# A decoder layer with soft experts on one core: unread products in TensorE's waits before the first expert, and one more copy for ScalarE

## The chip, the cores and the metric

The kernel runs on one core of a Trainium2 chip. The core has TensorE (PE, matrix products; its weight loads are listed apart as PEld), VectorE (DVE), ScalarE (ACT), GpSimd (POOL) and SyncE (SP, which issues most DMAs). Each works through its own queue in order, and they wait for each other through semaphores. The metric is the device time of one execution in microseconds (us), the median of several runs. Before the change it is 2900.55 us over 3 runs (2897.71 to 2901.32).

## The reference

A pre-norm decoder layer on x of 32 sequences x 100 tokens x 256 channels in float32, with a context of 361 tokens for each sequence:

```python
x = x + attn(layernorm(x))            # 16 heads of 16, rotary, causal
x = x + xattn(layernorm(x), ctx)      # 16 heads of 16, with biases, over 361 context tokens
x = x + ffn(layernorm(x))

# ffn: 8 experts of 128 slots each; two token softmaxes over the same logits
xn, sn = rmsnorm(x), rmsnorm(slot_embeds)
logits   = einsum('bnd,esd->bnes', xn, sn)
dispatch = softmax(logits, axis=tokens)
combine  = softmax(logits, axis=all 1024 slots)
slots = einsum('bnd,bnes->besd', xn, dispatch)
h     = gelu(einsum('besd,edh->besh', slots, w1) + b1)      # 256 -> 1024
eo    = einsum('besh,ehd->besd', h, w2) + b2                # 1024 -> 256
out   = einsum('bmd,bnm->bnd', eo, combine)
```

## The kernel before

The 32 sequences form 8 groups of 4 (SIZES). For each group and each of the 8 experts, `run_expert` computes `ph` (first layer, 16 products of 128x512), `hT` (gelu on ScalarE), `pe` (second layer, 32 pieces of products of 128x256) and `py` (the combination). While the experts of group g run, the attention work of group g+1 is threaded between their products. Group 0 has no experts to hide behind: its self attention, cross attention, logits and routing run alone ahead of the first `ph`. That is the part in which this change acts.

The order of all queues is written out when the program is built, by a planner inside the kernel. `pe["t"]` is its own clock for TensorE. `matmul` and `transpose` emit a product and call `spend`, which adds an estimated duration to `pe["t"]`, multiplied by `pe["slow"]`: 1.25 until group 0 is prepared, 1.0 behind that. Work for the other engines is queued as jobs (`vec`, `act`, `gps`, and `job("SP", ...)` for transfers) with an estimated duration, what they read and what they write. `run` emits every job that can start by `pe["t"]`, choosing by start time, priority and place in its list. The attention work is written as generators (`self_attention`, `cross_softmax`, `crossing`, `cross_queries`, `cross_context`, `prepare`, `slots`); each yields a `Need` with the tiles and PSUM banks that its next piece waits for. `drive` takes the next piece that fits; if none does, it calls `advance`, which moves `pe["t"]` on to the next event: that is a wait of TensorE as the planner sees it. `hold` does the same for a bank or tile that is needed at once.

PSUM: two score pairs, `sc0` and `sc1` (the ring "pairs", each of two banks of 512 columns; line 310), take turns for the score products of both attentions and for the transposed logits `ps_l` (line 1512). Self attention writes 400 columns of each bank, cross attention 361, `ps_l` all 512. Four single banks hold everything else until group 0 is prepared; after that they are split into two for attention and two for the experts (line 1805).

The names in the first part of the program, in the order of one sequence:

- `layer_stats` and `turned` (lines 659 and 692): bnst and bnmv on VectorE; ve, rstd and xh on POOL; `ps_xhT` transposes on TensorE, copied to xhT by ScalarE.
- self attention: `ps_qk` products, rope on VectorE and POOL (ropeu, ropet), rotk on ScalarE; score products sc<-rotk; p with the causal mask and nmax on VectorE, subtraction on POOL (line 891), exp on ScalarE (line 899); `ps_pT` transposes for group 0; `ps_av`, oT, `ps_o` into the residual x.
- context: `ps_cT` transposes, ctxT copies (ScalarE, line 1060), `ps_kT` products, kT (ScalarE, line 1076), `ps_xv` values into vpad (VectorE).
- cross attention in four "quads" for each sequence: score products sc<-kT,xqT into sc0 and sc1; xnmax on VectorE (line 1162, one reduction for each pair); exps on ScalarE (line 1172, two for each pair, each with an accumulator read). For group 0 (`early`) the exps go to p in SBUF, and `cross_turn` (line 1210) transposes p in three chunks of 128, 128 and 105 context tokens: 12 `ps_xpT` transposes for each quad, and one copy for each chunk into xpT. Chunk 1 is copied by ScalarE, chunks 0 and 2 by VectorE (line 1217). Later groups transpose through VectorE and a store and load in DRAM instead (xt, xd).
- `ps_rb`, `ps_xav`, xoT, `ps_o`; then `tokens` and `prepare`: `ps_lt` logits, `ps_l`, cnm, `ps_nm`; `soften` and `route`: pd, disp, sl, slT. Then the first `ph`.

The slot embeddings (se, 1 MB) are loaded at the start; eight squares on ScalarE (line 597), rn on POOL (line 603), a scaling on VectorE and 16 `ps_sn` transposes turn them into snT.

Of the kernel before, what the change touches and what calls it, by code (L numbers as in the profile page):

```python
# [23 lines left out]
def decoder_layer(ctx: ExitStack, tc: tile.TileContext, a: dict, out: bass.AP):  # L24
# [8 lines left out]
    nc = tc.nc  # L33
    x, cx = a["x"], a["ctx_1024"]
    B, S, D = x.shape
# [12 lines left out]
    HG = 4  # L48
# [28 lines left out]


    COL, PIPE, HOP, LOAD = 0.00084, 0.25, 0.15, 1.28
    pe = {"t": 0.0, "slow": 1.25}  # L80
    waiting = {e: [] for e in ("DVE", "ACT", "POOL", "SP")}
    idle_from = {"DVE": 0.0, "ACT": 3.0, "POOL": 5.0, "SP": 0.0}
    tables = {"now": None, "gelus": 0}
# [11 lines left out]
    class Buf:  # L95
# [2 lines left out]

        def __init__(self, make=None, prev=None, before=(), ap=None, root=None, psum=False):
            self.make, self.prev, self.before, self.ap, self.root = make, prev, before, ap, root  # L100
            self.psum = psum
            self.writes, self.uses = [], []

        def get(self):
# [86 lines left out]
    def ends(items):  # L191
        t = 0.0
        for i in items:
            e = i if isinstance(i, float) else i.end
            if e is None:
                return None
            t = max(t, e)
        return t
# [64 lines left out]
    def advance(*times):  # L263

        nxt = run()
        ahead = [t for t in (*times, nxt) if t is not None and t > pe["t"]]
        assert ahead, "nothing left that could go on"
        pe["t"] = min(ahead)

    def hold(items, fill=None):  # L270

        while True:
            run()
            t = ends(items)
            if t is not None and (t == 0.0 or t + HOP <= pe["t"]):
                return
            if fill is None or not fill():
                advance(None if t is None else t + HOP)

    def spend(cols, passes, share):  # L280
        pe["t"] += passes * (COL * cols / share + (0.012 if share > 1 else 0.0)) * pe["slow"]
# [15 lines left out]
    class Banks(Ring):  # L297
# [6 lines left out]
        def tile(self, name):  # L304
# [4 lines left out]
    rings = {  # L309
        "small": Banks([(ps_m, "mm"), (ps_b, "big")]), "big": None,  # L310
        "pairs": Kept(
            [ps_s.tile([P, 2, 512], F32, tag=f"sc{i}", name=f"sc{i}") for i in range(2)], psum=True
        ),
    }
# [26 lines left out]
    def free(when):  # L341
        return Need(banks=0, when=when)
# [27 lines left out]
    def drive(goal, *streams):  # L370


        while goal.it:
            run()
            ready = [s for s in streams if s.fits()]
            if ready:
                min(ready, key=lambda s: s.need.seq).step()
            else:
                advance(*(s.time() for s in streams))
        return goal.result  # L380

    ident = const.tile([P, P], F32, name="ident")
# [827 lines left out]
    def cross_turn(xpT, p):  # L1210
        for ci, (k0, n) in enumerate(KC):
            yield Need(*p)
            ps = bank("ps_xpT")
            for q in range(NQ):
                transpose(ps.get()[:n, q * SQ : (q + 1) * SQ], p[q].get()[:, k0 : k0 + n], ident)
            mine = xpT.part()
            f = nc.scalar.copy if ci == 1 else nc.vector.tensor_copy
            job(
                "ACT" if ci == 1 else "DVE", 0.49 if ci == 1 else 0.57,
                lambda f=f, ps=ps, n=n, ci=ci: f(  # L1220
                    xpT.get()[:n, :, ci, :, :QN],
                    ps.get()[:n].rearrange("k (h g u) -> k g h u", h=NQ, u=QB)[:, :, :, :QN],
                ),
                [ps], [mine], prio=0,
            )
# [235 lines left out]
    def prepare(g):  # L1461

        nb, nt = SIZES[g], SIZES[g] * S
        nm, cs, diag = R["cnm"].new(), R["cs"].new(), R["diag"].new()
        for b0 in range(0, nb, 2):
            m = min(2, nb - b0)
            for i in range(b0, b0 + m):
                yield free(lambda: len(turning) > 0)  # L1470
                k, at = turning.pop(0)
                assert at == i
                yield Need(k.xns[i])
                transposed(
                    k.xns[i], lambda: k.xn.get()[:, i, :],
                    lambda i=i: k.xnT.get()[:, :, i * S : (i + 1) * S], k.xnT,
                )
            yield free(lambda: state["slots"].it is None and state["routed"] >= NE - 1)
            if b0 == 0:
                k.logits()  # L1480
            cols_ = slice(b0 * S, (b0 + m) * S)
            for e in range(0, NE, 2):
                yield Need(k.xnT, snT)
                ps = bank("ps_lt")
                pv = ps.get().rearrange("p (e n) -> p e n", e=2)[:, :, : m * S]
                for i in range(2):
                    for dc in range(ND):
                        matmul(
                            pv[:, i, :], lhsT=snT.ap[:, dc, (e + i) * NS : (e + i + 1) * NS],
                            rhs=k.xnT.get()[:, dc, cols_],  # L1490
                            start=(dc == 0), stop=(dc == ND - 1),
                        )
                lt = k.lt[e // 2]
                act(
                    0.5, lambda lt=lt, pv=pv: nc.scalar.copy(lt.get()[:, :, cols_], pv), [ps], [lt],
                    prio=0,
                )
                vec(
                    0.57,
                    lambda e=e, pv=pv, ps=ps, b0=b0, m=m: nc.vector.tensor_reduce(  # L1500
                        k.mx.get()[:, e : e + 2, b0 : b0 + m],
                        pv.rearrange("m e (b n) -> m e b n", b=m), axis=AX.X, op=ALU.max,
                    ),
                    [ps], [k.mx], prio=0,
                )

            for b in range(b0, b0 + m):
                if g > 0 and b0 + 2 < nb:
                    mine = logit_squares(k, b, nm, cs)
                else:  # L1510
                    yield Need(*k.lt, banks=0, pairs=1, exps=(1.4, 4.0))
                    ps = rings["pairs"].new("ps_l")
                    pv = ps.get().rearrange("n h s -> n (h s)")
                    for e in range(NE):
                        transpose(
                            pv[:S, e * NS : (e + 1) * NS],
                            k.lt[e // 2].get()[:, e % 2, b * S : (b + 1) * S], ident,
                        )
                    warm("exp")
                    mine = nm.part()  # L1520
                    vec(
                        1.2,
                        lambda b=b, pv=pv: nc.vector.tensor_reduce(
                            nm.get()[:, b : b + 1], pv[:S], axis=AX.X, op=ALU.max, negate=True
                        ),
                        [ps], [mine], prio=0,
                    )
                    act(
                        1.28,
                        lambda b=b, pv=pv: nc.scalar.activation(  # L1530
                            pv[:S], pv[:S], AF.Exp, bias=nm.get()[:, b : b + 1],
                            accum_out=cs.get()[:, b : b + 1],
                        ),
                        [ps, mine], [cs.part()], table="exp", prio=0,
                    )
                vec(
                    0.27,
                    lambda b=b: nc.vector.tensor_scalar(
                        diag.get()[:, b, :], ident[:S, :S], nm.get()[:, b : b + 1], None, ALU.mult
                    ),  # L1540
                    [mine], [diag],
                )
        k.ci = R["cinv"].new()
        vec(
            0.18, lambda: nc.vector.reciprocal(k.ci.get()[:, :nb], cs.get()[:, :nb]), [cs], [k.ci]
        )

        yield Need(diag)
        ps = bank("ps_nm")
        matmul(  # L1550
            ps.get()[:, :nt], lhsT=ones, rhs=diag.get()[:, :nb].rearrange("k b n -> k (b n)"),
            start=True, stop=True,
        )
        k.nmB = R["nmB"].new()
        act(
            0.49, lambda: nc.scalar.copy(k.nmB.get()[:, :nt], ps.get()[:, :nt]), [ps], [k.nmB], prio=0
        )
# [222 lines left out]
    pe["t"] = 1.5  # L1780
    run()
    rows, se = load_constants()
    make_constants()
    load_slots(se)
    slots_kept.append(se.kept())
# [12 lines left out]
    def order():  # L1798
        return (*streams[:2], steps, *streams[2:])
# [14 lines left out]

    routing = Steps(routes(groups[0], 0))
    ready = drive(routing, routing, *order())
    w = weights
    todo = [(g, e) for g in range(NG) for e in range(NE)]
    for i, (g, e) in enumerate(todo):
# [115 lines left out]
```

## Time and profile before

| | |
|---|---|
| median of 3 runs | 2900.55 us (2897.71 to 2901.32) |
| profiled execution | 2904.49 us, its span 2902.5 us |
| mean granted TensorE clock | 0.987 of full speed |
| TensorE busy | 2855.3 us, 98% of the span |
| VectorE, ScalarE, POOL busy | 1519.4, 1190.6, 557.3 us (52%, 41%, 19%) |
| DMA | 446.34 MB, mean 154 GB/s |

TensorE's share is a mean over a short first part, in which one group's attention runs alone, and a long second part of experts. The costliest groups of the page are all of the second part. The columns are line, engine, operation, output and inputs, shapes, count; busy time and mean of one; idle time ahead of them:

```profile
L290 PE MATMUL pe<-w,hT 128*128 128x256 f32 x4096 | 980.4, 383 | 0.0
L290 PE MATMUL ph<-slT,w 128*128 128x512 f32 x2048 | 965.7, 598 | 0.5
L1693 ACT ACTIVATE hT<-ph,cols 128x512 f32<-128x512 f32 x512 | 351.7, 687 | 816.2 <-PE ph L290 816.0
```

The two lines of TensorE have no idle time of note ahead of them. What ended TensorE's waits in the first 254 us (us in total, times, longest):

```profile
PE ps_xhT L294 <- POOL xh L698: 7.0, 5, 4.3
PE psWk L294 <- DMA rawWk<-in_L_attn_Wk_dram: 5.8, 1, 5.8
PE sc L290 <- ACT p L1172: 4.5, 6, 1.5
PE sc L290 <- DVE xt L1186: 2.8, 2, 2.6
PE ps_xpT L294 <- ACT pT L934: 2.2, 1, 2.2
PE ps_rb L294 <- DVE wide L715: 2.1, 1, 2.1
PE ps_xpT L294 <- ACT kT L1076: 2.1, 1, 2.1
PE sc L290 <- DVE xqT L1122: 2.1, 1, 2.1
```

The waits are spread over many causes: ScalarE, VectorE, POOL and the first transfers.

### The profile page before, as it was taken

The page shows a single profiled execution, that of the slowest core. Times are in us where ns is not written, and L with a number is a line of the kernel's source. Part 1 is how long each engine was busy: PE and PEld are TensorE (multiplying, and loading weights), DVE is VectorE, ACT ScalarE, POOL GpSimd, SP SyncE. Part 2 cuts the span into 40 slices and gives each one's busy share as a digit, 9 for nine tenths or more (in the row PEclk, how much of TensorE's full clock was granted, in tenths as well). Part 3 has the DMA queues.
Part 4 walks back from the last instruction along what each step waited for, and adds up shares of the span by engine and source line. Part 5 has one row for each costly group of instructions (what it writes and reads, how often), then busy time and mean ns, then how long its engine had stood idle before and what let it go on. Part 6 is the DMA issues. An engine that isn't in the chain of part 4 may idle for free.

```text
span 2902.5 us, 42479 instructions
## 1 busy us (share of the span) xinstructions
PE 2855.3 (98%) x16609; PEld 1982.1 (68%) x16609; DVE 1519.4 (52%) x2831; ACT 1190.6 (41%) x2538; POOL 557.3 (19%) x729
## 2 busy tenths in 40 slices
PE   7989999999999999999999999999999999999999
PEld 5765667676667676676667667677666766676676
DVE  5676565565455556456465465555555555423121
ACT  3544444443434434444443444434434434333331
POOL 4331321022210322112220211202221021100000
PEclk8988999999999999999999999999999999999999
DMA  3015564555554554555464464554555455533231
GB/s 109 11 50 181 175 214 147 190 165 173 167 184 152 188 171 155 185 171 178 154 204 158 141 218 148 192 184 139 185 177 175 163 182 171 175 93 100 78 98 53
DMA packets 331542, 446.34 MB, mean 154 GB/s; under 512 B 18280, under 2 KB 300880, under 8 KB 331344
## 3 DMA queue, kind: packets, MB, share of 16 engines
q1 hardware_dynamic: 330656, 442.90, 46.8%
q8 instruction: 132, 2.16, 0.3%
q10 hardware_dynamic: 688, 0.73, 0.1%
q14 instruction: 66, 0.54, 0.1%
HBM read 300.82 MB, written 142.74 MB: 153 GB/s over the span
## 4 chain that ended last, share of the span: by engine, by line
PE 92%; DMA 3%; DVE 3%; ACT 1%; POOL 1%; issue 1%; SPq 0%; ACTq 0%; DVEq 0%; POOLq 0%
PE pe L290 30%; PE ph L290 30%; PE sc L290 5%; PE sl L290 4%; PE py L290 4%; PE ps_lt L290 3%; PE ps_xv L290 3%; PE ps_xav L290 2%; PE ps_kT L290 2%; PE ps_o L290 2%; PE ps_qk L290 2%; PE ps_av L290 1%; PE ps_v L290 1%; PE ps_xq L290 1%; DMA xpT<-xd 1%; PE ps_xpT L294 1%
## 5 line engine op out<-in xcount | busy, mean ns | idle before, releaser
L290 PE MATMUL pe<-w,hT 128*128 128x256 f32 x4096 | 980.4, 383 | 0.0
L290 PE MATMUL ph<-slT,w 128*128 128x512 f32 x2048 | 965.7, 598 | 0.5
L290 PEld LDWEIGHTS pe<-w,hT 128*128 128x128 f32 x4096 | 751.6, 190 | 159.3 <-issue 50.2
L1693 ACT ACTIVATE hT<-ph,cols 128x512 f32<-128x512 f32 x512 | 351.7, 687 | 816.2 <-PE ph L290 816.0
L290 PEld LDWEIGHTS ph<-slT,w 128*128 128x128 f32 x2048 | 372.0, 190 | 314.7 <-issue 285.5
L1172 ACT ACTIVATE sc<-sc,xnmax 128x361 f32<-128x361 f32 x448 | 238.0, 531 | 175.6 <-DVE xnmax L1162 168.2
L1162 DVE TENSOR_REDUCE xnmax<-sc 128x2 f32<-128x722 f32 x256 | 221.5, 899 | 167.9 <-PE sc L290 167.5
L1186 DVE STREAM_TRANSPOSE xt<-sc 128x384 f32<-128x384 f32 x448 | 230.5, 554 | 21.5 <-ACT sc L1172 15.1
L1592 POOL TENSOR_TENSOR dT<-dT,ri 128x400 f32<-128x400 f32 x64 | 54.9, 858 | 964.8 <-DVE ri L1589 964.8
L891 POOL TENSOR_TENSOR p<-p,nmax 100x800 f32<-100x800 f32 x64 | 96.7, 1523 | 421.3 <-DVE nmax L884 404.5
L1747 DVE SCALAR_TENSOR_TENSOR x<-py,cinv,x 100x256 f32<-100x256 f32 x256 | 112.0, 475 | 115.5 <-PE py L290 114.9
L667 POOL TENSOR_SCALAR ve<-bnmv 100x1 f32<-100x1 f32 x96 | 23.2, 244 | 724.3 <-DVE bnmv L664 674.2
L1724 DVE TENSOR_TENSOR eo<-pe,b 128x512 f32<-128x512 f32 x128 | 87.2, 681 | 137.9 <-PE pe L290 137.1
L290 PE MATMUL sc<-kT,xqT 32*128 32x361 f32 x1024 | 130.5, 532 | 9.5 <-ACT p L1172 4.5
L290 PEld LDWEIGHTS sl<-disp,xn 100*128 100x128 f32 x1024 | 134.4, 192 | 7.2 <-ACT sc L1172 0.6
L290 PE MATMUL sl<-disp,xn 100*128 100x128 f32 x1024 | 135.1, 275 | 0.0
L290 PE MATMUL py<-eo,cT 128*100 128x256 f32 x512 | 131.5, 379 | 0.8 <-DVE eo L1724 0.8
L290 PEld LDWEIGHTS py<-eo,cT 128*100 128x100 f32 x512 | 85.5, 167 | 50.0 <-issue 27.2
L874 DVE TENSOR_TENSOR p<-sc,causal 100x800 f32<-100x800 f32 x64 | 60.4, 985 | 106.2 <-PE sc L290 106.1
L811 DVE STREAM_TRANSPOSE st<-p 128x1024 f32<-128x1024 f32 x56 | 113.6, 2029 | 0.1
L1660 DVE TENSOR_SCALAR slT<-sl,cols 128x512 f32<-128x512 f32 x128 | 93.2, 728 | 37.7 <-PE sl L290 37.7
L1241 DVE TENSOR_TENSOR xoT<-ps_xav,rb 128x100 f32<-128x100 f32 x64 | 16.7, 260 | 180.9 <-PE ps_xav L290 180.8
(155 smaller groups left out, 3243.4 us busy)
## 6 DMA issues: line engine op xcount, KB each, us to landing
w<-in_L_ffn_w_dram SPq DMA_DIRECT2D x512, 256.0 KB
xd<-xt SPq DMA_DIRECT2D x112, 768.0 KB
xpT<-xd SPq DMA_DIRECT2D x112, 768.0 KB
sd<-st SPq DMA_DIRECT2D x70, 512.0 KB
pT<-sd SPq DMA_DIRECT2D x70, 512.0 KB
dd<-dt SPq DMA_DIRECT2D x56, 256.0 KB
disp<-dd SPq DMA_DIRECT2D x56, 256.0 KB
ctx<-in_ctx_dram SPq DMA_DIRECT2D x32, 256.0 KB
```

The costliest lines, as they stand in the source:

```text
L290: nc.tensor.matmul(out, lhsT=lhsT, rhs=rhs, **kw)
L811: lambda: nc.vector.transpose(st.get().rearrange("p j h u -> p h j u"), p.get()[:, hs, :].rearrange("p h (u j) -> p h j u", j=4),),
L874: lambda i=i, hs=hs: nc.vector.tensor_tensor(p.get()[:S, hs, :S].rearrange("n (q h) k -> n q h k", q=2), sc[i].get()[:S, :, : HG * S].rear ...
L891: lambda hs=hs: nc.gpsimd.tensor_tensor(p.get()[:S, hs, :S], p.get()[:S, hs, :S], nmax.get()[:, hs].unsqueeze(2).to_broadcast([S, HPC, S]) ...
L1162: lambda nm=nm, sc=sc: nc.vector.tensor_reduce(nm.get(), sc.get()[:, :, :SK], axis=AX.X, op=ALU.max, negate=True),
L1172: nc.scalar.activation(to[:, :SK], sc.get()[:, i, :SK], AF.Exp, bias=nm.get()[:, i : i + 1], accum_out=sums.get()[:, c, q, r : r + 1],)
L1186: nc.vector.transpose(t_.get()[:, :, :, 2 * t + i, :].rearrange("p j c u -> p c j u"), sc.get()[:, i, : NKB * P].rearrange("p (c u j) -> p ...
L1592: lambda: nc.gpsimd.tensor_tensor(dT.get()[:, :nb, :S], dT.get()[:, :nb, :S], ri.get()[:, :nb].unsqueeze(2).to_broadcast([P, nb, S]), ALU. ...
L1660: lambda dc=dc, sl=sl: nc.vector.tensor_scalar(slT.get()[:, dc, : nb * NS], sl.get()[:, : nb * NS], cols.ap[:, NGM + dc : NGM + dc + 1], N ...
L1693: lambda h=h, ph_=ph_, hc=hc: nc.scalar.activation(h.get()[:, :n], ph_.get()[:, :n], AF.Gelu, bias=cols.ap[:, e * NHC + hc : e * NHC + hc ...
L1724: lambda eo=eo, po=po, m=m: nc.vector.tensor_tensor(eo.get()[:, :m], po.get().rearrange("p (i d) -> p i d", i=2)[:, :m], b2.get().unsqueez ...
L1747: lambda b=b, i=i: nc.vector.scalar_tensor_tensor(xs[g].get()[:, b, :], py[:S, i, :], k.ci.get()[:, b : b + 1], xs[g].get()[:, b, :], ALU. ...
```

## The change

Three things are changed.

1. From the moment the constants are made until the first expert's routing is done (`awake`), `advance` hands each planned wait to `keep_awake`. It adds the waits up, and for each 0.4 us of them emits one product of the identity with 112 columns of itself into columns 400 to 511 of the second bank of sc0. Nobody reads these columns, except `ps_l` and its reader; while such a use of sc0 is not over (`whole`), nothing is emitted.
2. `pe["slow"]`, the planner's factor on TensorE's durations in that part, is 1.06 where it was 1.25.
3. In `cross_turn`, which only the first group uses, chunks 0 and 1 are copied by ScalarE and chunk 2 by VectorE.

```diff
-    pe = {"t": 0.0, "slow": 1.25}
+    pe = {"t": 0.0, "idle": 0.0, "slow": 1.06}
...
-            self.psum = psum
+            self.psum, self.whole = psum, False
...
         assert ahead, "nothing left that could go on"
+        keep_awake(min(ahead) - pe["t"])
         pe["t"] = min(ahead)
+
+    def keep_awake(wait):
+
+
+        if not awake:
+            return
+        now = rings["pairs"].past[::2][-1:]
+        if now and now[0].whole and (ends(now[0].uses) or 1e9) > pe["t"]:
+            return
+        pe["idle"] += wait
+        while pe["idle"] > 0.4:
+            nc.tensor.matmul(
+                rings["pairs"].tiles[0][:, 1, HG * S :], lhsT=ident, rhs=ident[:, : 512 - HG * S],
+                start=True, stop=True,
+            )
+            pe["idle"] -= 0.4
...
+    awake = []
...
-            f = nc.scalar.copy if ci == 1 else nc.vector.tensor_copy
+            f = nc.scalar.copy if ci < 2 else nc.vector.tensor_copy
             job(
-                "ACT" if ci == 1 else "DVE", 0.49 if ci == 1 else 0.57,
+                "ACT" if ci < 2 else "DVE", 0.49 if ci < 2 else 0.57,
...
                     ps = rings["pairs"].new("ps_l")
+                    ps.whole = True
...
     rows, se = load_constants()
+    awake.append(True)
     make_constants()
...
     ready = drive(routing, routing, *order())
+    awake.clear()
     w = weights
```

## The prediction

> **What bounds the kernel now.** I read the page's shares and slices first, then a table by stage, then the places where TensorE ran at half clock, then the waits ahead of them. The slices (40 of 72.6 us each):
>
> ```profile
> PE   7989999999999999999999999999999999999999
> ...
> PEclk8988999999999999999999999999999999999999
> ```
>
> TensorE is short of 9 tenths, and its granted clock below full, in the first slices alone. The table by stage has, for each stretch, its length, then busy time of PE, weight loads, DVE, ACT and POOL, then the clock, DMA share and GB/s. The first row is everything up to the first expert's steady run, the second the rest:
>
> ```profile
> 0.00:254.00 254.00, 215.36 (x1719) 156.64 (x1720) 169.70 (x324) 114.52 (x316) 89.96 (x127) 0.86 0.24 75
> 254.00:2902.50 2648.50, 2639.92 (x14892) 1825.49 (x14890) 1349.69 (x2507) 1076.08 (x2222) 467.29 (x602) 1.00 0.49 161
> ```
>
> After 254 us TensorE idles 2648.50 - 2639.92 = 8.6 us at full clock. Nothing that this change does can gain there. Before it TensorE idles 254.00 - 215.36 = 38.6 us, and part of its busy time is at half clock. Half-microsecond windows give ten such stretches (length, PE busy, clock, DMA share, GB/s):
>
> ```profile
> 29.15:32.50 3.35, 3.01 (x6) 0.50 0.09 30
> 35.95:42.75 6.80, 6.28 (x33) 0.50 0.00 0
> 53.00:59.75 6.75, 6.12 (x31) 0.50 0.01 2
> 63.25:66.65 3.40, 2.86 (x14) 0.50 0.00 0
> 70.05:80.35 10.30, 10.30 (x36) 0.50 0.01 2
> 141.75:145.10 3.35, 3.35 (x20) 0.50 0.00 0
> 148.55:155.40 6.85, 6.85 (x24) 0.50 0.00 0
> 182.70:189.50 6.80, 5.89 (x65) 0.50 0.18 61
> 216.95:237.35 20.40, 17.56 (x76) 0.50 0.53 183
> 244.15:247.50 3.35, 3.29 (x50) 0.50 0.38 92
> sum 71.35, PE 65.50; mean PE 6.55
> ```
>
> The lengths are multiples of about 3.4 us: the clock is set by such windows. At full clock the 65.50 us would be 32.75. So 32.75 us is the most that a warm TensorE can give. The same work shows the ratio (8 products ps_qk each, cold, then warm):
>
> ```profile
> 56.79 1.92 PE L290 MATMUL ps_qk<-xhT,wTWk 128*128 128x100 f32 x8
> ...
> 110.89 1.06 PE L290 MATMUL ps_qk<-xhT,wTWk 128*128 128x100 f32 x8
> ```
>
> Ahead of each fall stands a wait of TensorE:
>
> ```profile
> 36.47 0.59 PE L294 MATMUL ps_xhT<-ident,xh 100*128 100x100 f32 x2 [4.31 <-POOL xh L698]
> 51.51 0.39 PE L294 MATMUL ps_xhT<-ident,xh 100*128 100x100 f32 x2 [1.86 <-POOL xh L698]
> 63.79 2.82 PE L294 MATMUL ps_xpT<-ident,p 128*128 128x128 f32 x12 [2.19 <-ACT pT L934]
> 147.45 0.88 PE L290 MATMUL sc<-kT,xqT 32*128 32x361 f32 x4 [1.13 <-ACT p L1172]
> 201.64 0.39 PE L294 MATMUL ps_xhT<-ident,xn 100*128 100x100 f32 x2 [0.58 <-POOL xn L1441]
> ```
>
> The 1.13 us were enough for the fall at 148.55; the 0.58 us at 201 were not. In this trace the edge lies between some 0.6 and 1.1 us of idleness in 3.4 us.
>
> **The change, part by part.** I count in the built programs' orders of instructions.
>
> *Products that nobody reads.* 146 are added, in 44 runs, all ahead of the first expert's second sl. The price of one: 8 ps_qk of 128x100 start 0.98 us apart (109.91 to 110.89), 0.12 us each warm; cold 1.85/8 = 0.23 (56.79 to 58.64). A product of 128x112 on 128 weights is nearest to that. The planner books 0.4 us for each but TensorE issues them back to back, so a run fills about 0.12/0.4 = 30% of a planned wait when warm and 58% when cold. 26 stand before the first ps_qk and 18 in the wait that the page shows as 4.31 us. The first 9 wait for a memset of sc that ends at 5.47 us and take 1.1 us, so psWk starts at 6.6 instead of 5.80; 11 more make the first ps_xhT about 1 us late. This costs nothing: the load of se lands at 26.9, eight squares and then rn (33.44) and xh (35.09) on POOL follow it, and TensorE idles 1.88 and 4.31 us under it. If that cover were gone it would cost about 1.5 us.
>
> What they may save: from 29.2 to 247.5 us TensorE idles 218.30 - 189.80 = 28.5 us, and the 120 products there are 120 x 0.12 = 14.4 us, half of it. Half of a 2 us wait left idle is at the edge found above, so I go stretch by stretch. In full: the fall at 29.15, whose wait (ctxT, 1.88 us) goes because the ctx transposes now stand ahead of the self scores; at 35.95 (18 products, 2.2 to 4.1 us of 4.31); at 53.00 (runs of 6, 3, 4 and 4): (3.01 + 6.28 + 6.12)/2 = 7.7 us. At half credit, with runs of 1 to 8 near the same place: 63.25, 70.05, 148.55, 182.70 and 216.95: (2.86 + 10.30 + 6.85 + 5.89 + 17.56)/4 = 10.9 us. None: 141.75 (2 to 3 products in 2 us of wait) and 244.15 (the filling is switched off by then). Sum 18.6 us of TensorE time; bounds 0 and 32.75.
>
> How much of it the end sees: in the cold stretches the chain of waits runs through TensorE (from 70 to 80 and 148.5 to 155 wholly), but at their ends it changes to ScalarE, VectorE or POOL, whose work does not get faster. I take three quarters, 14.0 us.
>
> The Trainium skill ("TensorE: Matmul & The Clock Gate", section "Why this matters for your kernels") asks for no TensorE gaps over about 3 us between bursts; by that only the 4.31 us wait needs filling, and the sum would be 6.28/2 x 3/4 = 2.4 us before costs, that is no gain worth the name. The rows above disagree (1.13 us sufficed), and I go by them.
>
> *What the products hold up.* They write the second bank of the first score pair, and in the built order 24 of the 44 runs wait for a VectorE or ScalarE reader (or the memset) of it, and 22 such readers wait for a product. Behind the run wait TensorE's next real products; behind the reader, the exps. First, a run that ends late: half a product, 0.06 us, for the 38 runs after the start: 2.3 us (0 if always early; 24 x 0.90 = 21.6 us if each run held TensorE for a whole xnmax reduction of 0.90 us). Mostly the next real product waits for the same reader or one later in the same queue, so I take the low value. Second, a reader behind a product: 0.12 for it and about 0.1 for each of two hand-overs (the xnmax pair of 1.72 us from 60.13 has its first half done near 60.99, the exp starts at 61.08), 0.3 us; 22 x 0.3 = 6.6 us, of which a fifth on the path, since xnmax (6.7%) and exps (4.8%) are 11.5% of the chain of waits from 29 to 247 us, doubled for caution: 1.3 us (0 to 6.6).
>
> *Two of three xpT copies on ScalarE.* 16 copies of 0.57 us leave VectorE (9.2 us) and cost ScalarE 16 x 0.52 = 8.3 us. ScalarE is busy 103.55 of the 218.30 us, VectorE 153.96, so it goes to the emptier engine. Against it: TensorE waited 4.5 us for exps (six times) and two waits of 2.1 us for other ScalarE work, and behind a copy stand the next exps. For it: two pairs of xpT copies on VectorE stand on the chain (173.72 and 179.14, 0.96 us). Bounds: -3 us (six copies off the path) and +4 (eight exps late by 0.51). I take 0.
>
> *The planner's slowness 1.06 for 1.25.* It emits no instruction. It reorders all queues before the first expert: half of one ctx's transposes, two score products and their two exps move behind it, one reciprocal, its widening and a slT copy ahead. On SP one ctx load goes ahead of three w2 loads that nobody needs before 254 us, and one dd store ahead of the first ph; POOL keeps its count and swaps xh and p steps. Behind the first expert's start the orders are nearly the same (7760 of 7769 TensorE instructions match, 1104 of 1105 DMAs, all 608 of POOL). I take 0, bounds -4 and +4 (two waits of some 2 us come or go).
>
> *Sum:* -14.0 + 2.3 + 1.3 = -10.4 us. The profiled execution took 2904.49 us (span 2902.5 and 2.0 around it), 3.9 above the median of 2900.55; taken off it, 2894.1; on the median's scale 2900.55 - 10.4 = 2890.
>
> **The rivals.** 0.2% is 5.8 us, about what can be told from no change.
>
> Rival A, the clock stays up nearly everywhere: all but the last stretch saved, (65.50 - 3.29)/2 = 31.1 us, four fifths seen, 24.9, less 3.6: 2879. For it: fewer cold windows also end sooner, since a warm run needs less. Against: waits of 2 us with one or two products.
>
> Rival B, too few products: 30% filled leaves over 1 us idle in most windows, and the clock falls as before outside the start. A quarter saved: 32.75/4 x 3/4 = 6.1, less 3.6: 2898. For it: the planner's 0.4 against 0.12. This is also the case that the change doesn't do what it says.
>
> Rival C, slower: the shared bank. TensorE, in order, stands at a product until VectorE's reduction of the score pair has ended, while real products behind it are ready, and the exps wait for the next product. Full price 21.6 + 6.6 = 28.2 us against 14.0 saved: +14, 2915; it decides from half of that price on. For it: 24 runs do carry such waits. Against: most real products behind them wait on the same queue.
>
> **How the numbers follow.** Forecast 0.47 (gain of 6 to 17 us; own range 2883 to 2895), A 0.18, B 0.16, C 0.19. Forecast and A are faster by over 0.2%: 0.65. B is within 0.2%: 0.16; C slower: 0.19. The range 2871 to 2909 takes in A with the reordering's 4 us and the copies' 3, and C up to some three quarters of its price; about a tenth is left out above and less below.
>
> **What would show it.** The clock of the first 254 us above 0.86 (0.93 by the forecast, 0.98 by A, under 0.90 by B), the first expert's ph starting some 10 us earlier than at 241.02, no cold stretch between 36 and 42.75. C would show as waits of the added products on DVE xnmax or ACT p of over 10 us in total. ScalarE as the releaser of more than the 4.5 us of score waits would show that the copies hurt. The prediction is wrong if TensorE's saved time turns into waits for POOL and ScalarE, or if the tail after the first expert changes by more than 4 us.

## The result and the profile after

The changed kernel takes 2924.4 us (median of 4 runs, 2920.65 to 2930.59), the kernel before 2899.13 beside it (4 runs, 2889.65 to 2901.32). The ratio is 1.0096 with a 95% interval of 1.0067 to 1.0124: about 28 us slower. The profiled execution took 2930.59 us, its span is 2928.6 us. The prediction was 2890.

The slices of the page (73.2 us each) show nothing: TensorE's first slice is at 8 tenths, where it was at 7. The table by stage (length; PE, weight loads, DVE, ACT, POOL busy; clock; DMA share; GB/s), as before the change:

```profile
0.00:254.00 254.00, 223.31 (x1901) 177.84 (x1902) 152.85 (x289) 112.15 (x311) 87.22 (x123) 0.90 0.21 64
254.00:2928.60 2674.60, 2660.16 (x15002) 1837.35 (x15001) 1358.35 (x2527) 1085.81 (x2244) 470.59 (x606) 1.00 0.49 161
```

In the first 254 us the clock rose from 0.86 to 0.90 and TensorE is busier by 8 us, yet VectorE did less there than before: 152.85 us in place of 169.70, of which the copies that moved to ScalarE are at most 9.2. The stage is late, not busy. The first `ph` starts at 264.26 us in place of 241.02. Before the change, then after it:

```profile
241.02 1.04 PE L290 MATMUL ph<-slT,w 128*128 128x512 f32 x2
```

```profile
264.26 1.91 PE L309 MATMUL ph<-slT,w 128*128 128x512 f32 x2
```

From there to the end 2928.6 - 264.3 = 2664.3 us pass (before 2902.5 - 241.0 = 2661.5). So all but some 3 us of the loss is made ahead of the first expert.

The waits up to 262 us, first TensorE's at products (`sc L281` is the unread product), then those of other engines for products. The columns are the engine, what waits, what it waits for, total, times, longest:

```profile
PE sc L281 <- ACT p L1191: 7.2, 7, 1.3
PE sc L281 <- DVE xnmax L1181: 6.6, 8, 1.4
...
PE sc L281 <- DVE xt L1205: 2.4, 2, 1.2
...
ACT p L1191 <- PE sc L281: 13.0, 7, 4.2
DVE xnmax L1181 <- PE sc L281: 9.8, 6, 3.9
ACT sc L1191 <- PE sc L281: 7.0, 2, 5.6
DVE xt L1205 <- PE sc L281: 4.5, 2, 4.2
```

Neither kind can exist in the kernel before. With the smaller rows (two of TensorE's of 2.2 and 2.1 us, one of VectorE's of 1.8) TensorE stands 20.5 us at products for readers of sc0, and readers of sc0 stand 36.1 us for products. Such a figure is the whole idle time that a product's end closed, so it also holds time in which the reader waited for other things. How one place looks, in the timeline (start, duration, engine, line, operation, and in brackets the idle time ahead and what ended it):

```profile
55.48 0.89 PE L309 MATMUL sc<-kT,xqT 32*128 32x361 f32 x8
...
56.82 1.72 DVE L1181 TENSOR_REDUCE xnmax<-sc 128x2 f32<-128x722 f32 x2
...
57.77 0.70 PE L281 MATMUL sc<-ident 128*128 128x112 f32 x4 [1.39 <-DVE xnmax L1181]
...
58.50 0.56 ACT L1191 ACTIVATE p<-sc,xnmax 128x361 f32<-128x361 f32 x1 [1.14 <-PE sc L281]
...
59.75 1.19 PE L281 MATMUL sc<-ident 128*128 128x112 f32 x4 [1.29 <-ACT p L1191]
...
63.96 0.91 DVE L1181 TENSOR_REDUCE xnmax<-sc 128x2 f32<-128x722 f32 x1 [3.92 <-PE sc L281]
...
65.80 0.56 ACT L1191 ACTIVATE p<-sc,xnmax 128x361 f32<-128x361 f32 x1 [4.16 <-PE sc L281]
```

The scores of a pair have two readers in turn, the reduction and the exps. The planner put a product between them. So the product waits for the reduction, the exps wait for the product, the next product for the exps, the next reduction for that product. Three engines take turns where they overlapped. Of the 3.92 us ahead of the reduction at 63.96 the product itself adds only the last 0.7: the scores that it reduces (61.66, 1.57 us) end at 63.23. These scores are late in their turn, behind the products at 59.75 and 61.07. The 1.39 and 1.29 us for which TensorE now stands idle are also such as the prediction found ahead of falls of the clock: the products at 57.77 take 0.70 us for x4, those at 59.75 take 1.19, and the granted clock is 0.99 from 56 to 59 us and 0.50 from 59 to 70.

### The profile page after: what moved, and what is told of

Read it like the earlier page. It is cut to its first block, busy times and chain, and to the rows that moved or that the text cites. A ratio compares the mean times of both kernels' runs of the same rounds, so it can differ in the third digit from the quotient of the medians.

```text
span 2928.6 us, 43045 instructions
## 1 busy us (share of the span) xinstructions
PE 2883.5 (98%) x16901; PEld 2015.2 (69%) x16901; DVE 1511.2 (52%) x2815; ACT 1198.0 (41%) x2555; POOL 557.8 (19%) x729
## 4 chain that ended last, share of the span: by engine, by line
PE 93%; DMA 3%; DVE 3%; ACT 1%; issue 0%; POOL 0%; SPq 0%; DVEq 0%; ACTq 0%; POOLq 0%
PE ph L309 29%; PE pe L309 29%; PE sc L309 5%; PE sl L309 4%; PE py L309 4%; PE ps_xv L309 3%; PE ps_lt L309 3%; PE ps_kT L309 3%; PE ps_xav L309 3%; PE ps_qk L309 2%; PE ps_o L309 2%; DMA xd<-xt 1%; PE sc L281 1%; PE ps_av L309 1%; PE ps_v L309 1%; PE ps_xq L309 1%
```

## The experiments

"Over before" is the ratio to the kernel before, less 1, times 2900 us; both ran on the same chip side by side. The "lost clock" is (1 - mean granted clock) x span, a mean over the runs; the clock has three digits, so one run's is good to about 3 us. The waits are from one profile each, summed up to 262 or 270 us, without the first product's wait for a memset.

### The parts

`e2_no_fill` keeps the planner's slowness and the copies and emits no product. The products don't move the planner's clock, so the order of all real work is that of the changed kernel:

```diff
     rows, se = load_constants()
-    awake.append(True)
```

> The changed kernel without the unread products; the order of all other work is the same as in the changed kernel. W: the loss goes, 2893 to 2907 us. O: it stays, 2916 to 2928.

`e1_fill_only` has the products, with slowness 1.25 and the copies as before:

```diff
-    pe = {"t": 0.0, "idle": 0.0, "slow": 1.06}
+    pe = {"t": 0.0, "idle": 0.0, "slow": 1.25}
...
-            f = nc.scalar.copy if ci < 2 else nc.vector.tensor_copy
+            f = nc.scalar.copy if ci == 1 else nc.vector.tensor_copy
```

> The unread products alone, with slowness 1.25 and the copies as before: 113 products in 34 runs, 16 of which wait for work of VectorE or ScalarE on the same bank, and 8 readers wait for a product. Theory W (the waits on the shared bank make the loss): about half of the loss, 2905 to 2914 us. Theory O (the new order from 1.06 and the moved copies makes it): as before or faster, 2885 to 2902.

Without products 2898.35 us (ratio 0.9989, 0.9973 to 1.0005), with products in the old order 2906.05 (1.0027, 1.0015 to 1.0040). So the products are the whole loss, 26 us of median (31 by the ratios), and cost less where the order puts fewer readers behind them: 8 in place of 22, with 7.9 us of readers' waits in place of 36.1.

`e5_slow_only` and `e6_copies_only` are the kernel before with one of the other two edits:

> The kernel before with the planner's slowness 1.06 alone, no products, copies as before. Both edits without products took 2898.4. If neither does anything: 2897 to 2902. Rival, two effects that cancel: 2893 to 2896 or 2902 to 2905, with the copies alone on the other side of 2900.

> The kernel before with two of three copies of the transposed probabilities on ScalarE alone, no products, the planner's slowness as before. If neither edit does anything: 2897 to 2902. Rival, two effects that cancel: on the other side of 2900 from the slowness alone, by 3 to 5 us.

2895.97 us (0.9990, 0.9979 to 1.0001) and 2894.70 (0.9986, 0.9971 to 1.0000). Both are a hair low, neither is told from no change, and they don't cancel one another.

### Is it the waits or the products' size?

`e3_tiny_fill` keeps every product in its place with its waits, and cuts it to one weight column and one data column:

```diff
-                rings["pairs"].tiles[0][:, 1, HG * S :], lhsT=ident, rhs=ident[:, : 512 - HG * S],
+                rings["pairs"].tiles[0][:1, 1, HG * S : HG * S + 1], lhsT=ident[:, :1], rhs=ident[:, :1],
```

> The changed kernel with each unread product cut to one column of weights and one column of data: the same places and the same waits, nearly no work. W: slow as the change, 2915 to 2930 us. If TensorE's time for the products makes the loss (146 at some 0.24 us, 35 us, partly in waits): 2895 to 2908. O: 2916 to 2928, so e2 and e3 together tell it.

`e4_free_fill` puts a product only into a score pair whose readers have ended by the plan:

```diff
+        free = [
+            i for i in range(2)
+            if not (now := rings["pairs"].past[i::2][-1:])
+            or (ends(now[0].uses) or 1e9) + HOP <= pe["t"]
+        ]
+        if not free:
+            return
```

> The changed kernel, but a product is only emitted into a score pair that by the plan no reader uses (either pair), else left out: 71 products in 24 runs, 8 of them with some wait, no reader waits for one. W: no loss, 2885 to 2905 us. O: 2912 to 2926.

Tiny products: 2916.32 us (1.0057, 1.0037 to 1.0077). So the places and their waits cost most of it, with next to no work: a tiny product takes some 0.05 us (36 of them in a row take 1.94 us in `e10_tiny_free`, below). Part of this price is the clock, which these waits make colder (38.6 us lost, 31.3 without products). Free pairs: 2900.01 (1.0000, 0.9989 to 1.0011): products without a reader behind them cost nothing and give nothing, though there are only 71.

### Which of the two waits?

`e7_behind_readers` emits a product only where all readers of the pair's last scores already stand in their queues; the product may wait for them, but none can wait for it. `e9_before_readers` takes the other products:

```diff
+        # e7
+        if now and (not now[0].uses or ends(now[0].uses) is None):
+            return
...
+        # e9
+        if not now or not now[0].uses or ends(now[0].uses) is not None:
+            return
```

> The changed kernel, but a product is put down only where all readers of the pair's last scores already stand in their engines' queues: 111 products in 38 runs, 17 of which wait for a reader, and no reader waits for a product (in the changed kernel 146 in 44, 24 and 22; with products into free pairs alone 71 in 24, 8 and 0, which took 2900.0 us). Theory R, the price lies in the readers that stand behind a product: 2899 to 2906 us. Rival L, it lies in TensorE standing at a product for a reader that is late: 9 of the 16 added waits of the changed kernel are here, so some 9/16 of 24 us, 2911 to 2917. Rival N, each product costs by itself: 26 us x 111/146 on 2898.4, 2918.

> The other half of the changed kernel's products: only where a reader of the first score pair's last scores is not yet in its engine's queue, so that it comes behind the product. 35 products in 15 runs, 10 of which wait for an earlier reader, and 19 readers wait for a product. The products of the other half alone took 2900.4, the changed kernel 2924.4, neither half 2898.4. Theory R, the price lies in the readers behind a product: 19/22 of 24 us, 2915 to 2924, and waits of VectorE and ScalarE for products of over 20 us in total. Rival J, the price comes only from the two kinds together, or from the number of products: 2899 to 2908.

`e13_behind_tiny` and `e14_before_tiny` are the same two with products of one column:

> The 111 products that no reader stands behind, cut to 1 weight column and 1 data column: the same places and waits, no length, no heat. In full they took 2900.4 at a mean lost clock of 19.8 us; no products 2898.4 at 31.3. Theory L, their own length of some 12 us is on the path and their warmth pays it back: without both 2897 to 2901, lost clock 29 to 34. Rival W, TensorE's waits at them are the cost and the warmth paid for those: 2906 to 2912.

> The 35 products that 19 readers stand behind, cut to 1 weight column and 1 data column. In full 2910.0. Theory R, the readers' waits cost: 2905 to 2910. Rival L, the products' length costs, 35 times 0.23 us or 8 us: 2898 to 2903.

| kernel | products | TensorE at products, us | readers for products, us | lost clock, us | median, us | over before, us (interval of the ratio) |
|---|---|---|---|---|---|---|
| no products (e2) | 0 | 0 | 0 | 31.3 | 2898.35 | -3 (0.9973 to 1.0005) |
| behind readers, full (e7) | 111 | 16.3 | 0 | 19.8 | 2900.43 | +1 (0.9993 to 1.0012) |
| behind readers, tiny (e13) | 111 | 15.8 | 0 | 28.2 | 2897.63 | -2 (0.9981 to 1.0007) |
| before readers, full (e9) | 35 | 7.0 | 27.6 | 30.3 | 2910.05 | +11 (1.0023 to 1.0054) |
| before readers, tiny (e14) | 35 | 7.9 | 19.5 | 34.5 | 2908.13 | +12 (1.0029 to 1.0058) |
| all, tiny (e3) | 146 | 20.9 | 25.5 | 38.6 | 2916.32 | +17 (1.0037 to 1.0077) |
| all, full (changed kernel) | 146 | 20.5 | 36.1 | 28.5 | 2924.40 | +28 (1.0067 to 1.0124) |

Theory R holds in the main: the loss comes where readers wait, not with the number of products, and 16 us of TensorE's own waits at products cost nothing that can be told. It is not in proportion to the readers' waits: e9 has 27.6 us of them for +11, e3 25.5 for +17. And one kind of wait is not separated: TensorE's waits on xnmax (5.6 us in e9, 5.9 in e14) stand at the same products as the readers' waits, and e7 has none of them. Taken wholly as loss they would be some 40% of what these kernels take over no products (14 and 15 us), so the readers' waits remain the larger part. The 35 products that readers stand behind cost 11 to 12 us over before, whether they are full or tiny; e9 came out under what was expected (2915 to 2924), and its profile is that of its fastest run, 2904.45. The place shown above, in e7:

```profile
56.70 1.72 DVE L1183 TENSOR_REDUCE xnmax<-sc 128x2 f32<-128x722 f32 x2
...
57.64 0.56 ACT L1193 ACTIVATE p<-sc,xnmax 128x361 f32<-128x361 f32 x1 [0.39 <-DVE xnmax L1183]
...
58.88 0.70 PE L283 MATMUL sc<-ident 128*128 128x112 f32 x4 [2.62 <-ACT p L1193]
...
61.68 2.16 PE L315 MATMUL ps_xpT<-ident,p 128*128 128x128 f32 x12
```

The exp starts 0.39 us after its engine is free, with the reduction, and the product waits 2.62 us behind the exps. The next real product, `ps_xhT`, could not go on much earlier: POOL ends its input xh at 58.53 us. The transposes `ps_xpT` start at 61.68 us, in the changed kernel at 67.14, without products at 58.99. Counted from the start of the reduction xnmax (56.70, 56.82 and 54.21) that is 4.98, 10.32 and 4.78 us: here e7 loses 0.2 us, the changed kernel 5.5.

With tiny products the halves add up within their intervals: against no products 1 + 15 us beside 20 for all. With full products they don't: 4 + 14 beside 31, so 13 us come only with the two kinds together, as rival J had it for the whole. In the changed kernel the full products lengthen the readers' waits from 25.5 to 36.1 us: once readers wait for TensorE, the length of each product ahead of them in its queue is on their path too. That is read from the waits and fits the 11 us between the last two rows; no run isolates it.

### Is the warmth worth anything?

`e8_dense_free` fills free pairs with a product for each 0.2 us of planned wait, and `e10_tiny_free` cuts these products to one column:

```diff
-        while pe["idle"] > 0.4:
+        while pe["idle"] > 0.2:
...
-            pe["idle"] -= 0.4
+            pe["idle"] -= 0.2
```

> Products only into a pair whose readers have ended, with one product for each 0.2 us of planned wait in place of 0.4: 142 products in 25 runs, 8 waiting, no reader behind one. Theory (waits are the price, the products' own work is not): 2896 to 2902 us, with a mean granted clock at or over the 0.991 of the run with 71 products; if a microsecond less of lost clock is worth some 0.8 us, a lost clock of 20 us in place of 25.5 would bring 2896. Rival N, each product costs by itself: 142/146 of 26 us, 2923. Rival D, a denser filling overshoots the real waits (142 products of 0.23 us are 33 us, of which 37 products stand in the waits of the start that cost nothing): 2905 to 2910.

> The dense filling of free pairs (142 products, no reader behind one), each cut to 1 weight column and 1 data column: the same places and the same orders, no heat and almost no length. The full products took 2899.3 at a mean lost clock of 15.2 us, against 31.3 without products (2898.4). Theory G, what a product's warmth saves its length and its overshoot give back: 2897 to 2902 at a lost clock of 28 to 33. Rival H, a microsecond of lost clock costs 0.8 us here too, and something else held the full products back: 2909 to 2914. Rival P, the length is on the path and warmth is worth nothing: 2888 to 2893.

2899.33 us (1.0002, 0.9989 to 1.0015) at a lost clock of 15.2, and 2896.80 (1.0002, 0.9990 to 1.0013) at 27.8. (e10 came out a little under its expectation in both numbers.) So 142 products can be had for nothing, within about 5 us, which is what the two intervals leave, and the clock does become warmer, by 12.6 us of lost clock, but the time stays. That fits theory G: what the warmth saves, the products' length gives back. A case that the expectations don't name, length in idle time and warmth off the path, would give the same time. Two readings speak for G. The length is on the path at the start: the 36 products ahead of the second sequence's first transposes take 8.19 us in e8 and 1.94 in e10, and these transposes start at 43.06 us in e8, 36.74 in e10 and 34.37 without products. And the warmth seems to count: over e8's own 12 runs the time rises by 0.61 us for each microsecond of lost clock (correlation 0.83), over e10's by 0.63 (0.71), so 12.6 us would be worth some 8 by this estimate. No run isolates either side of the cancellation.

The last four ask for a better version: only the start filled (up to 40 us of the planner's time), in the new order (e11) and in the old order with the copies (e12); only what comes behind 40 us, without a reader behind it, in the new order (e15) and in the old one with the copies (e16).

```diff
-        if not awake:
+        if not awake or pe["t"] > 40:
```

> The dense filling of free pairs only up to 40 us of the planner's time, where the waits for the first loads and for the slot embeddings are long: 97 products in 10 runs, 2 waiting, no reader behind one. If filling pays in long waits and is given back in short ones: 2892 to 2897. If the long waits' end is set by transfers and the clock behind them falls anyway: 2897 to 2901. If the first products make the first weights' transposes late (psWk at some 10 us in place of 5.8): over 2902.

> The same filling of the start (82 products in 9 runs), with the planner's slowness of before and the two copies on ScalarE, which alone took 2894.7 (2888.5 to 2905.4). If the start's filling saves the early fall of the clock: 2888 to 2893, below both kernels. If it saves nothing: 2893 to 2898.

> The products that no reader stands behind, without those before 40 us of the planner's time: 62 in 28 runs. Against no products, the 49 of the start moved the second sequence's first transposes from 34.37 to some 36.5 us, because the score products of the first sequence and POOL's subtraction stand behind them too. If this 2 us is all that they do: 2897 to 2899. If their warmth counted for more: 2901 to 2904.

> The same late filling without a reader behind it (42 products in 17 runs) on the planner's order of before with two copies on ScalarE, which alone took 2894.7. If filling that holds no reader up saves anything at all: 2888 to 2893, below both kernels. If length and warmth cancel: 2893 to 2898. If it costs: over 2898.

| kernel | median, us | ratio to before |
|---|---|---|
| e11, start only | 2902.70 | 1.0014 (1.0001 to 1.0026) |
| e12, start only, old order, copies | 2901.30 | 1.0018 (1.0006 to 1.0030) |
| e15, late only | 2901.65 | 1.0006 (0.9993 to 1.0018) |
| e16, late only, old order, copies | 2895.79 | 0.9999 (0.9988 to 1.0010) |

Filling the start costs 4 to 5 us over before, 7 to 9 over the same order without products (e2 0.9989, e6 0.9986). The first weights' transposes, psWk, start at 11.52 us in e11 and 12.57 in e12, in place of 5.57 without products: e11 ended in the branch that named this (over 2902), e12 above all of its own. e15 missed its expectation of 2897 to 2899; beside e7 (1.0002) it can't be told whether dropping the start helped. No filling beats the kernel before. The lowest ratio of all is that of the copies alone, 0.9986, whose interval touches 1.

What the start's products delay in the changed kernel: the second sequence's first transposes start at 34.37 us without products and at 36.48 in the changed kernel. Two of POOL's steps ahead of it, without products and then in the changed kernel:

```profile
27.51 3.00 POOL L910 TENSOR_TENSOR p<-p,nmax 100x800 f32<-100x800 f32 x2 [8.86 <-DVE nmax L903]
...
31.33 1.65 POOL L622 TENSOR_TENSOR rn<-n,mhalf 128x8 f32<-128x8 f32 x1
```

```profile
28.97 4.17 PE L281 MATMUL sc<-ident 128*128 128x112 f32 x36
...
29.61 3.01 POOL L910 TENSOR_TENSOR p<-p,nmax 100x800 f32<-100x800 f32 x2 [8.34 <-DVE nmax L903]
...
33.44 1.65 POOL L622 TENSOR_TENSOR rn<-n,mhalf 128x8 f32<-128x8 f32 x1
```

POOL works in order, and its subtraction on the first sequence's scores stands ahead of rn. These scores come from TensorE, behind the first products, and are 2.1 us later. These are single profiles: the others of this order without products at the start have the transposes at 33.99 to 34.36 us (e5, e9, e14) and at 35.88 (e15, where the first `ps_kT` products take 3.80 us in place of 2.64), those with the start filled much alike at 36.26 and 36.77 (e4, e7).

## Why the prediction was wrong, step by step

- *The part before the first expert alone can change*: right. From the first `ph` to the end it is 2664.3 us beside 2661.5; over the profiles of the experiments this stretch varies from 2658.7 to 2666.1.
- *What the products hold up, 2.3 + 1.3 us*: this is the step that failed. It found the 24 runs and the 22 readers, gave the range up to 21.6 + 6.6, and took the low end of both: half a product for each run, since the next real product mostly waits for the same reader; 0.3 us for each reader, a fifth of it on the path. For the runs it was right as far as is shown: e7's 16.3 us of such waits cost nothing that can be told, but none of them is on xnmax, and the 6.6 us on xnmax are not separated from the readers' waits. For the readers it was wrong in size: 36.1 us of idle time closed by a product, where 6.6 were counted for hand-overs and products, because a product doesn't come right behind the reduction but when TensorE's queue gets to it, often behind another product that waits too (4.16 us for one exp). And in share: the tiny products, nearly all waits, cost about 20 us (e3 against e2, the colder clock included), not 1.3. The share of an engine in the chain of waits of before did not tell its share in the chain that the change makes.
- *The price of a product, 0.12 us*: wrong by half. The trace lists two entries for each of these products: the 18 in the wait at 29 us are x36 above and take 4.17 us, 0.23 each at full clock. The 8 ps_qk entries that the price came from were 4 products. 146 products are thus 34 us, not 17.5. In the two small terms of the sum this changes little (half of 0.23 us for 38 runs and a fifth of 0.43 for 22 readers, 4.4 + 1.9 us in place of 2.3 + 1.3); what it would have changed in the 18.6 us is open. The 9 products at the very start took still longer, 4.15 us (x18, 0.46 each) and not 1.1, so psWk started at 9.57 us and not at 6.6.
- *The start costs nothing under the load of se*: wrong by 2.1 us against the same order without products. The cover was taken to be the load and the squares; the other input of POOL's queue, the scores, was missed. Against the profile of the kernel before it came out even (36.48 beside 36.47). Whether the new order brought these 2 us is not shown: in the old order the same transposes start at 33.73 us in e6's profile and at 36.63 in e16's, neither with products at the start.
- *18.6 us saved at the clock, three quarters of it seen, 14.0*: not seen. The stage's clock rose to 0.90, not 0.93, which fits that the waits for readers made TensorE idle again (in e7, where no reader waits, it is 0.92); over the runs the lost clock is 28.5 us in the changed kernel against 31.3 without products. Where no reader is held up, it falls to 19.8 or 15.2, and even then nothing is left in the time.
- *The edge at some 0.6 to 1.1 us of idleness, against the Trainium skill's 3 us* ("TensorE: Matmul & The Clock Gate", section "Why this matters for your kernels"): for the clock the rows were the better guide. Filling the start alone, where the long waits are, leaves 24.9 us of lost clock (e11); filling the shorter waits behind it as well leaves 15.2 (e8). For the time it made no difference that can be told. Idleness does not account for all of it: the prediction's rows at 70.05 and 148.55 us are at half clock with TensorE busy throughout (10.30 and 6.85 us), which no run explains.
- *Copies and slowness, 0 each*: right, within what can be told (0.9986 and 0.9990).
- *Rival C, the shared bank, 2915, chance 0.19*: this is what happened, with the sign that its own check named: over 10 us of waits of products on xnmax and p (6.6 + 7.2). The sign alone did not tell the price, though: e7 has 9.9 us of waits on p and loses nothing. Its larger part was misplaced: it put 21.6 of its 28.2 us on TensorE standing at products and 6.6 on the readers, and it is mainly the readers that cost; that its 28.2 us are near the measured 26 is luck. Its point of decision, half of the price on the path, was passed. The count of 22 readers behind products, known beforehand, spoke for it and was weighed too low.

## What to carry to other kernels

An instruction that does nothing useful still takes part in the order of everything that touches its buffer. Count both directions before pricing it: a filler that waits for a reader can be free where the next real work waits too, a reader that waits for a filler lengthens the chain by the filler's whole place in its queue. Put fillers only into a buffer whose readers are done or already queued, and try them at one column first: that shows the price of the waits without that of the work.

And a warmer clock is no gain by itself: where the filler's length stands in the same chain, it can take back what the warmth saves, as e8 and e10 suggest. Here no filling beat the kernel without it.

## What the hardware showed beside this

The runs of the kernel before spread over 18.5 us (2892.1 to 2910.6, 25 runs beside the first four experiments), and the granted clock tells which is which: at 0.986 they took 2907.1 to 2910.6 us, at 0.992 2893.7 to 2897.8. A line through them gives 0.82 us for each microsecond of lost clock (correlation 0.91). So the time of the same program goes with how much of it falls into half clock in a run, and two or three runs are few for a question of 0.3%. Such a slope is a correlation between runs of one kernel. It does not price a clock warmed by fillers: between e8 and e10 it would make some 10 us of 12.6 us of lost clock, and the time is the same.
